# A transformer block, two spectral layers and a scan on one core: attention in query blocks of 464 columns, and position terms along w from slices of one table

## The chip, the core and the metric

The kernel runs on one core of a Trainium2 chip. TensorE (PE) multiplies matrices; VectorE (DVE), ScalarE (ACT) and GpSimd (POOL) work on elements; SyncE (SP) issues most of the transfers (DMA). The metric is the time of one execution on the device, in microseconds (us), lower is better. An f32 matrix product shows in the profile as two MATMUL instructions, a bf16 one as one.

## The reference, cut to what matters

The input is an image of 48 x 48 tokens with 768 channels, all f32. Four layers follow one another: an attention block with an MLP, a spectral mixing layer, a scan, and a second spectral layer. Only the attention of the first is touched:

```python
qkv = xn.reshape(B, H * W, C) @ qkv_w + qkv_b          # 12 heads of 64
attn = jnp.einsum('bqc,bkc->bqk', q * scale, k)         # 2304 x 2304 for a head
coords = jnp.arange(H)[:, None] - jnp.arange(H)[None, :] + (H - 1)
Rh = rel_pos_h[coords]
Rw = rel_pos_w[coords]
rel_h = jnp.einsum('bhwc,hkc->bhwk', r_q, Rh)
rel_w = jnp.einsum('bhwc,wkc->bhwk', r_q, Rw)
attn = (attn.reshape(B * nh, H, W, H, W) + rel_h[:, :, :, :, None] + rel_w[:, :, :, None, :])
attn = jax.nn.softmax(attn.reshape(B * nh, H * W, H * W), axis=-1)
out = jnp.einsum('bqk,bkc->bqc', attn, v)
```

The position term along w takes, for a query in column w, the dot product of q with 48 rows of a table of 95: `rel_pos_w[w - k + 47]`. For all queries of one column it is the same 48 rows, a window of the table that moves by one row from column to column. The term along h is built in the same way.

## The kernel before, in words

`qkv_phase` (L181) makes q, k and v for three superblocks (sb) of 768 tokens. For each superblock, `v_rows` makes v, then `q_and_k` (L268) goes over six pairs of heads (pr), each with seven matrix products of 128 x 128 weights (`wqk`, loaded from DRAM by `load_qk`, L243, for the second and third superblock), and stores q and k to DRAM on ACT's queue (L327).

Beside these runs the work on position terms, `position_terms` (L382). It is a list of steps, 24 for a superblock: twelve h steps (`rel_h`, L407), then twelve w steps (`rel_w`, L392). A step makes four products of 96 moving columns into one PSUM tile, and `split` (L367) turns it into three bf16 parts: ACT copies the first part (L371), VectorE subtracts (L372), ACT copies the second part (L373), VectorE subtracts (L374). The weights of each step are a table of 192 KB, `relD`, loaded by `tables` (L376); it holds for each of four positions a 128 x 96 block-diagonal matrix, so that one full-array product serves both heads of a pair. When the parts of a superblock are complete, `store` (L388) writes them to DRAM (`rw_d`, `rh_d`); the tiles `rw` and `rh` have one buffer each.

`advance` (L434) runs one step, and keeps the loads of the next ones ahead of it. It is called twice in each of the pairs 2 to 5 of `q_and_k` (L323; that makes the first eight h steps), and between the products of v of the next superblock (`between`, L444; the other sixteen). The third superblock has no v after it: its last sixteen steps run at the end, where a bound on the scores is computed as well (L461 to L478, ending in `flag`, by which the attention chooses between two programs; here it always takes `attention_bounded`). Four steps stand after the bound, then the pools of the projections are closed (`inner.close()`), five more follow, then `ahead(1)` opens the attention's buffers and loads its first block, and the rest of the steps follows. `ahead(0)`, which loads the one-hot table and the keys and values of the first pair of heads, stands after pair 1 of the last superblock (L329).

`attention_bounded` (L526) goes over six pairs of heads, for each over six blocks of 384 queries, for each over 18 tiles of 128 keys, in groups of three key tiles (`KB`). A group issues on TensorE, in this order: the products of keys and queries for its three tiles (L559; the two heads use the upper and the lower 64 rows of the array), the position terms added to them by a product with a 0/1 matrix `oneh` (L567, bf16, 120 rows), and the values of the group before (L588; the two heads use the left and the right 64 columns). ACT takes the exponential of each tile for both heads (L569), VectorE adds up the row sums (L574, L577). At the end of a block the sums are added over partitions (L595), inverted (L597) and multiplied in (L603). `load_bias` (L489) loads a block's position terms, with eight transfers for a pair of heads, and `load_chunk` loads q besides; two blocks are held (`qbs`). Every seventh group one step of `weight_sums` (L742) is run: it loads weights of later stages through SP, adds them on POOL and stores them. It borrows buffers from the pool of probabilities (`p`, ten buffers).

The instructions of an engine run in the order in which they are queued. The framework may place an instruction earlier or later than its line in the program, as long as what it depends on is done; SP's queue shows it most.

Of the kernel before, what the change touches and what calls it, by code (L numbers as in the profile page):

```python
# [20 lines left out]
P = 128  # L21
# [9 lines left out]
NTB = T // TB  # L31
LN_EPS = 1e-5
# [148 lines left out]
def qkv_phase(tc, ident, x, qkv_w, qkv_b, relT, rel_d, ln_g, ln_b, q_d, k_d, v_d, rw_d, rh_d, wqk_d, wv_d, flag, home, ahead):  # L181
# [18 lines left out]
    with (  # L200
# [67 lines left out]
        def q_and_k(sb, have_q, step):  # L268
# [4 lines left out]
            for pr in range(NC):  # L273
# [55 lines left out]
                if pr == 1 and sb + 1 == NSB:  # L329
                    ahead(0)  # L330
# [9 lines left out]
        with tc.tile_pool(name="qkv_v0", bufs=1, side="right") as vp:  # L340
            w = vp.tile([P, 7, NC2, TB], F32, tag="wv", name="wv")
            a21 = vp.tile([P, NC2, TB], F32, tag="a21", name="a21")
            load_x(0, 0)
            for k in range(2):
                nc.sync.dma_start(w[:, k], wv[:, k * NC2 : (k + 1) * NC2, 2 * C : 2 * C + TB])
            prepare(0, 0)
            load_x(0, 1)
            nc.sync.dma_start(w[:, 6], wv[:, NC2:, 2 * C + TB :])
            nc.sync.dma_start(a21, wv[:, :NC2, 2 * C + TB :])
            vb = load_bcast(nc, kp, qkv_b[2 * C : 3 * C], C, "vb")  # L350
            qkb = load_cols(nc, kp, qkv_b[0 : 2 * C], 2 * NC, "qkb")
            kb = kp.tile([P, NC], F32, tag="kb", name="kb")
            rel = qp.tile([P, 2, 2 * G - 1], F32, tag="rel", name="rel")
            for s in range(2):
                nc.sync.dma_start(rel[s * HD : (s + 1) * HD], relT)
            qms, kms = (qp.tile([P, NC, NSB], F32, tag=n, name=n) for n in ("qms", "kms"))
            prepare(0, 1)
            combine(nc.gpsimd, (w[:, 0], w[:, 1], a21, w[:, 6]), w[:, 3], w[:, 2], w[:, 5], w[:, 4])
            sums(0)
            V.tensor_scalar(kb, qkb[:, NC : 2 * NC], HD**-0.5, None, ALU.mult)  # L360
            v_rows(0, lambda n: w[:, n])
            nc.sync.dma_start(wv_d, w)

        with tc.tile_pool(name="qkv_o", bufs=1, side="right") as op:
            R = 2 * G

            def split(ps, parts, n):  # L367

                r = op.tile([P, TB], F32, tag="rest", name=f"rest_{n}", bufs=2)
                r = r[:R].rearrange("p (a b c) -> p a b c", a=ps.shape[1], b=ps.shape[2])  # L370
                nc.scalar.copy(parts[0], ps)  # L371
                V.tensor_tensor(r, ps, parts[0], ALU.subtract)  # L372
                nc.scalar.copy(parts[1], r)  # L373
                V.tensor_tensor(parts[2], r, parts[1], ALU.subtract)  # L374

            def tables(which, g, n):  # L376

                d = qp.tile([P, 4, R], F32, tag="relD", name=f"relD_{which}_{g}_{n}", bufs=4)
                nc.sync.dma_start(d, rel_d[which, g])
                return d  # L380

            def position_terms(sb, q):  # L382
# [5 lines left out]
                def store(d, at, cols):  # L388
                    for s in range(2):
                        nc.sync.dma_start(d[s, :, :, sb, cols], at[s * G : (s + 1) * G].rearrange("k n c b t -> k n (c b t)"))  # L390

                def rel_w(g):  # L392

                    if g == 0:
                        tiles["rw"] = op.tile([P, 3, NC, 2, TB], BF16, tag="rw", name=f"rw_{sb}")
                    d, at = tiles.pop(("w", g)), tiles["rw"]
                    ps = pm.tile([P, 512], F32, tag="m", name=f"rw_{sb}_{g}")
                    pv = ps[:R, :TB].rearrange("p (c b w h) -> p c b w h", c=NC, b=2, w=4)
                    j, w0 = divmod(4 * g, KTW)
                    for i in range(4):  # L400
                        nc.tensor.matmul(pv[:, :, :, i, :], lhsT=d[:, i, :], rhs=q6[:, :, :, j, w0 + i, :], start=True, stop=True)
                    cols = slice(j * P + w0 * KTH, j * P + (w0 + 4) * KTH)
                    split(ps[:R, :TB].rearrange("p (c b t) -> p c b t", c=NC, b=2), [at[:R, n, :, :, cols] for n in range(3)], f"w{sb}_{g}")
                    if g == G // 4 - 1:
                        store(rw_d, at, slice(0, NC * TS))

                def rel_h(cp, n, hh):  # L407
# [10 lines left out]
                    if (n, hh) == (1, 1):  # L418
                        store(rh_d, at, slice(2 * cp * TS, (2 * cp + 2) * TS))

                def load(key, *args):
                    tiles[key] = tables(*args, "_".join(str(k) for k in (sb, *key)))

                for cp in range(NC // 2):
                    for n in range(2):
                        for hh in range(2):
                            key = "h", cp, n, hh
                            steps.append((lambda key=key: load(key, 0, 2 * (2 * sb + key[2]) + key[3]), lambda key=key: rel_h(*key[1:])))
                for g in range(G // 4):
                    steps.append((lambda g=g: load(("w", g), 1, g), lambda g=g: rel_w(g)))  # L430
# [21 lines left out]
            for sb in range(NSB):  # L452
# [6 lines left out]
                q_and_k(sb, lambda q: position_terms(sb, q), advance)  # L459

# [4 lines left out]
            V.tensor_reduce(rm, rel, axis=AX.X, op=ALU.max, apply_absolute_value=True)  # L465
# [13 lines left out]
            for _ in range(4):  # L479
                advance()  # L480
            inner.close()
            for _ in range(5):
                advance()
# [5 lines left out]
def load_bias(nc, bt, rw_d, rh_d, h, blk):  # L489

    c, s = divmod(h, 2)
    nw = 3 * KTW
    sb, n = divmod(blk, 2)
    cols = slice((2 * c + n) * TB, (2 * c + n + 1) * TB)
    w = rw_d[s].rearrange("(j k) n b f -> j (k n) b f", j=KJ)[:, :, sb, cols].rearrange("j r t -> r j t")
    r = rh_d[s].rearrange("(a k) n b f -> a (k n) b f", a=2)[:, :, sb, cols]
    for a in range(2):
        nc.sync.dma_start(bt[:nw, a], w)
        nc.sync.dma_start(bt[nw:NBR, a], r[a].unsqueeze(1).to_broadcast([NBR - nw, KJ, TB]))
# [9 lines left out]
def attention_loads(nc, q_d, k_d, v_d, rw_d, rh_d):  # L509
# [7 lines left out]
    def chunk(qb, c):  # L517
        pr, qc = c
        nc.sync.dma_start(qb[0], q_d[pr * P : (pr + 1) * P, qc * TB : (qc + 1) * TB])
        for s in range(2):  # L520
            load_bias(nc, qb[1][:, s], rw_d, rh_d, 2 * pr + s, qc)
# [4 lines left out]
def attention_bounded(tc, ahead, oT, beside, load_next):  # L526
# [12 lines left out]
    QB = TB  # L539
    KB = 3  # L540
    (load_keys_values, load_chunk), kvs, qbs, ones, oneh = ahead
    with (
# [9 lines left out]
        probs, scs = {}, {}  # L552

        def products(c, kt):
            pr, qc = c
            ps = ps_s.tile([P, 2, 512], F32, tag="s", name=f"s_{pr}_{qc}_{kt}")
            for s in range(2):
                rows = slice(s * HD, (s + 1) * HD)
                nc.tensor.matmul(ps[:, s, :QB], lhsT=keys[pr % 2][rows, kt * P : (kt + 1) * P], rhs=qbs[qc % 2][0][rows], start=True, stop=False)  # L559
            scs[c, kt] = ps  # L560

        def scores(c, kt):
            pr, qc = c
            b, j = divmod(kt, KJ)
            ps = scs.pop((c, kt))
            for s in range(2):
                nc.tensor.matmul(ps[:, s, :QB], lhsT=oneh[:NBR, b % 3, :], rhs=qbs[qc % 2][1][:NBR, s, b // 3, j, :], start=False, stop=True)  # L567
            p = pp.tile([P, 2, QB], F32, tag="p", name=f"p_{pr}_{qc}_{kt}")
            nc.scalar.activation(p, ps[:, :, :QB], AF.Exp)  # L569
            probs[c, kt] = p  # L570

            if kt == 1:
                acc = rp.tile([P, 2, QB], F32, tag="acc", name=f"acc_{pr}_{qc}")
# [7 lines left out]
        def values(c, kt):  # L581
# [4 lines left out]
            for s in range(2):  # L586
                rows = slice(s * HD, (s + 1) * HD)
                nc.tensor.matmul(avs[c][rows, :QB], lhsT=vals[pr % 2][:, kt, rows], rhs=p[:, s, :], start=kt == 0, stop=kt == NT - 1)  # L588

        def row_sums(c):  # L590
            pr, qc = c
            acc = probs.pop(c)
            rs = ps_v.tile([P, 512], F32, tag="rs", name=f"rs_{pr}_{qc}")
            for s in range(2):
                nc.tensor.matmul(rs[s * HD : (s + 1) * HD, :QB], lhsT=ones, rhs=acc[:, s, :], start=True, stop=True)  # L595
            rec = rp.tile([P, QB], F32, tag="rec", name=f"rec_{pr}_{qc}")
            nc.vector.reciprocal(rec, rs[:, :QB])  # L597
            recs[c] = rec

        def finish(c):  # L600
            pr, qc = c
            av, rec = avs.pop(c), recs.pop(c)
            nc.vector.tensor_tensor(oT[:, pr, qc * QB : (qc + 1) * QB], av[:, :QB], rec, ALU.mult)  # L603

        work = [((pr, qc), k0) for pr in range(NC) for qc in range(T // QB) for k0 in range(0, NT, KB)]
        other = beside(op, lambda name: pp.tile([P, 2, QB], F32, tag="p", name=name))
        for i in range(len(work) + 1):
            if i % 7 == 3:
# [3 lines left out]
            if i < len(work):  # L612
                c, k0 = work[i]
                pr, qc = c
                if k0 == 0:
                    nxt = (pr, qc + 1) if qc + 1 < T // QB else (pr + 1, 0)
                    if nxt[0] < NC:
                        load_chunk(qbs[nxt[1] % 2], nxt)
# [18 lines left out]
def attention_any(tc, ident, oneh, q_d, k_d, v_d, rw_d, rh_d, oT, beside, load_next):  # L637
# [9 lines left out]
    with (  # L647
# [13 lines left out]
        for h in range(NH):  # L661
# [5 lines left out]
            for i in range(NTB):  # L667
                load_bias(nc, bt[:, :, :, i * TB : (i + 1) * TB], rw_d, rh_d, h, i)
# [623 lines left out]
def block_kernel(ctx: ExitStack, tc: tile.TileContext, a: dict):  # L1292
# [25 lines left out]
    def load_ahead(stage):  # L1318
# [7 lines left out]
        qbs = [(pool.tile([P, TB], F32, tag=f"qt{i}", name=f"qt{i}"), pool.tile([P, 2, 2, KJ, TB], BF16, tag=f"bt{i}", name=f"bt{i}")) for i in range(2)]  # L1326
# [462 lines left out]
def laid_out(i):  # L1789
# [9 lines left out]
    rel = np.zeros((2, G, 2, HD, 2 * G), np.float32)  # L1799
    for pos in range(G):  # L1800
        for s in range(2):
            rel[:, pos, s, :, s * G : (s + 1) * G] = d["relT"].transpose(1, 0, 2)[:, :, G - 1 - pos : 2 * G - 1 - pos]
    d["relD"] = rel.reshape(2, G // 4, 4, P, 2 * G).transpose(0, 1, 3, 2, 4)
# [34 lines left out]
```

## Time and profile before

| | |
|---|---|
| median of three runs | 3839.18 us (3835.62 to 3842.34) |
| the profiled execution | 3837.04 us |
| its span, first to last instruction | 3835.2 us |
| mean granted TensorE clock | 0.987 |
| projections and position terms (0 to 514 us) | 513.8 us |
| attention (514 to 1688 us) | 1174 us |
| position terms along w, MATMUL of L401 | x288, 32.6 us busy |
| position terms along h, MATMUL of L415 | x288, 55.8 us busy |

In the profile's group lines, a group is named by line, engine and operation, then output<-input by the program's names, the shape and the count; after the bar come the busy time in us and the mean of one instruction in ns, and after the second bar the idle time of the engine just before them, with what ended it. PEld is the weight load that goes with a MATMUL. A MATMUL's duration includes the way through the array, so two that follow each other overlap; the rate is read from start to start. In the timeline a line has the start, the time to the end of the last of the instructions merged in it, and in square brackets the idle time before it and what ended that. SPq lines are transfers as they are issued. The chain is the sequence of work that ended last.

### The profile page before, as it was taken

Reading aid. Unit: us, or ns where it says so; the run is one execution under the profiler, and the core shown is the slowest. Engines: PE = TensorE matmul, PEld = TensorE weight load, DVE = VectorE, ACT = ScalarE, POOL = GpSimd, SP = SyncE. Lnnn points to the kernel's source line nnn. Section 1 sums busy time; section 2 is a strip of 40 time slices with the busy share of each in tenths; the row PEclk is TensorE's granted clock in tenths of the full one; section 3 lists DMA queues with packets and bytes.
Section 4 is the critical chain, followed back from the end, with each engine's and each line's share of the span. In section 5 each row is a group of like instructions: output and inputs, shape, how many; then the busy total and the mean of one; then the engine's idle time right before and its main releaser. Section 6 shows DMA issues by size and latency. Waiting matters only on the chain.

```text
span 3835.2 us, 54419 instructions
## 1 busy us (share of the span) xinstructions
PE 3726.5 (97%) x22018; PEld 2254.6 (59%) x22018; DVE 2058.8 (54%) x3184; ACT 1146.8 (30%) x1911; POOL 655.8 (17%) x498
## 2 busy tenths in 40 slices
PE   8999979999999999999999999999999998999998
PEld 4666544444444444445555555555558876996685
DVE  6655456666666666555524332323325567995455
ACT  1322234444444444420310121012013356223342
POOL 3101001111111111015000000000013310982131
PEclk9999989999999999999999999999999999999999
DMA  7656563333232322124434533443453412112345
GB/s 256 213 188 192 180 186 120 112 105 126 87 114 76 113 77 91 42 71 133 154 107 137 173 104 114 136 146 105 124 160 102 113 41 94 36 36 73 97 116 154
DMA packets 267834, 460.43 MB, mean 120 GB/s; under 512 B 33053, under 2 KB 220373, under 8 KB 261079
## 3 DMA queue, kind: packets, MB, share of 16 engines
q1 hardware_dynamic: 257767, 435.93, 37.2%
q10 hardware_dynamic: 9808, 20.94, 1.5%
q8 instruction: 175, 2.87, 0.3%
q14 instruction: 84, 0.69, 0.1%
HBM read 318.49 MB, written 138.31 MB: 119 GB/s over the span
## 4 chain that ended last, share of the span: by engine, by line
PE 90%; DVE 3%; DMA 2%; POOL 2%; ACT 1%; issue 1%; SPq 0%; ACTq 0%; DVEq 0%; POOLq 0%
PE p L867 13%; PE p L930 13%; PE s L559 12%; PE av L588 12%; PE s L567 6%; PE qk L295 6%; PE c L1094 4%; PE c L1187 3%; PE v L164 3%; PE pj L164 2%; PE f_z L1497 2%; PE f_z L1498 2%; PE f_x L1462 2%; PE so L1272 2%; PE f_u L1512 2%; PE rh L415 1%
## 5 line engine op out<-in xcount | busy, mean ns | idle before, releaser
L577 DVE TENSOR_TENSOR acc<-acc,p 128x768 f32<-128x768 f32 x576 | 583.9, 1014 | 353.9 <-ACT p L569 315.7
L569 ACT ACTIVATE p<-s 128x768 f32<-128x768 f32 x648 | 478.5, 812 | 693.8 <-PE s L567 581.3
L930 PE MATMUL p<-w,h 128*128 128x384 f32 x1512 | 492.7, 486 | 0.0
L559 PE MATMUL s<-qt,kv 64*128 64x384 f32 x2592 | 478.5, 502 | 9.9 <-ACT p L569 7.7
L588 PE MATMUL av<-p,kv 128*64 128x384 f32 x2592 | 464.5, 493 | 0.0
L930 PEld LDWEIGHTS p<-w,h 128*128 128x128 f32 x1512 | 286.2, 190 | 196.9
L559 PEld LDWEIGHTS s<-qt,kv 64*128 64x128 f32 x2592 | 233.1, 187 | 250.6 <-ACT p L569 116.3
L588 PEld LDWEIGHTS av<-p,kv 128*64 128x64 f32 x2592 | 170.0, 136 | 225.2 <-issue 216.1
L867 PE MATMUL p<-x2nT,w 128*128 128x384 f32 x864 | 292.7, 488 | 3.9 <-POOL rr L906 3.9
L295 PE MATMUL qk<-xnT,wqk 128*128 128x384 f32 x756 | 252.4, 491 | 5.2 <-DMA wqk<-wqk_d 5.2
L1187 PE MATMUL c<-H,bands 128*48 128x96 f32 x5632 | 243.8, 247 | 11.1 <-issue 10.9
L567 PE MATMUL s<-bt,oneh 120*128 120x384 bf16 x1296 | 249.2, 329 | 0.0
L1187 PEld LDWEIGHTS c<-H,bands 128*48 128x48 f32 x5632 | 235.6, 124 | 19.5 <-issue 11.3
L867 PEld LDWEIGHTS p<-x2nT,w 128*128 128x128 f32 x864 | 164.8, 191 | 119.2 <-POOL rr L906 4.1
L867 PE MATMUL p<-xT,w 128*128 128x384 f32 x648 | 220.8, 486 | 0.0
L567 PEld LDWEIGHTS <-oneh 120*128 120x128 bf16 x1296 | 109.3, 98 | 174.6 <-issue 116.1
L295 PEld LDWEIGHTS qk<-xnT,wqk 128*128 128x128 f32 x756 | 144.6, 193 | 99.9 <-issue 8.5
L906 POOL TENSOR_TENSOR rr<-rr,ml_b 128x1152 f32<-128x1152 f32 x12 | 31.9, 2660 | 955.6 <-DMA rr<-xr_d 864.4
L862 ACT ACTIVATE h<-h,ml_b 128x384 f32<-128x384 f32 x144 | 88.4, 615 | 345.8 <-DVE h L882 174.3
L1195 POOL TENSOR_TENSOR t<-s,c 128x768 f32<-128x768 f32 x80 | 144.7, 1834 | 178.8 <-DMA bands<-in_bands_dram 169.1
L867 PEld LDWEIGHTS p<-xT,w 128*128 128x128 f32 x648 | 123.1, 190 | 85.9
L597 DVE RECIPROCAL rec<-rs 128x384 f32<-128x384 f32 x36 | 92.1, 2558 | 100.7 <-PE rs L595 100.7
(322 smaller groups left out, 4803.7 us busy)
## 6 DMA issues: line engine op xcount, KB each, us to landing
w<-w1s_d SPq DMA_DIRECT2D x36, 768.0 KB
w<-w2s_d SPq DMA_DIRECT2D x36, 768.0 KB
bt<-rh_d SPq DMA_DIRECT2D x144, 162.0 KB
w<-w1s_d SPq DMA_DIRECT2D x36, 576.0 KB
w<-in_mlp_w_dram SPq DMA_DIRECT2D x27, 768.0 KB
wqk<-wqk_d SPq DMA_DIRECT2D x12, 1344.0 KB
yu<-f_ys SPq DMA_DIRECT2D x24, 672.0 KB
bt<-rw_d SPq DMA_DIRECT2D x144, 108.0 KB
```

Of the source, the lines that this page charges most:

```text
L164: nc.tensor.matmul(p[:, :TB], lhsT=rhs[n][:, c, t * P : (t + 1) * P], rhs=w[:, c, :], start=c == 0, stop=c == NC2 - 1)
L295: nc.tensor.matmul(p[:, :TB], lhsT=w[:, n, c, :], rhs=ops[sb][n][:, c, :], start=c == 0, stop=c == NC2 - 1)
L559: nc.tensor.matmul(ps[:, s, :QB], lhsT=keys[pr % 2][rows, kt * P : (kt + 1) * P], rhs=qbs[qc % 2][0][rows], start=True, stop=False)
L567: nc.tensor.matmul(ps[:, s, :QB], lhsT=oneh[:NBR, b % 3, :], rhs=qbs[qc % 2][1][:NBR, s, b // 3, j, :], start=False, stop=True)
L569: nc.scalar.activation(p, ps[:, :, :QB], AF.Exp)
L577: nc.vector.tensor_tensor(probs[c], probs[c], p, ALU.add)
L588: nc.tensor.matmul(avs[c][rows, :QB], lhsT=vals[pr % 2][:, kt, rows], rhs=p[:, s, :], start=kt == 0, stop=kt == NT - 1)
L867: nc.tensor.matmul(p[:, :TB], lhsT=w[n][:, c, :], rhs=rhs[n][:, c, :], start=c == 0, stop=c == NC2 - 1)
L930: nc.tensor.matmul(ps[t][:, :TB], lhsT=hs[left, f][:, t * P : (t + 1) * P], rhs=wt[:, f % KW2, :], start=f == 0, stop=f == NF2 - 1)
L1094: nc.tensor.matmul(ps[:K, i, :n], lhsT=v[:, c, tok : tok + K], rhs=w[:, cc, c0 : c0 + n], start=cc == NC - 1, stop=cc == 0)
L1187: nc.tensor.matmul(ps[r0 : r0 + G, k // 4, cols], lhsT=bands[:, n - GC, i, :] if gr else bands0[:, n, i, :], rhs=H[:, n, :, d : d + NPR], ...
L1195: GP.tensor_tensor(t, sc[:, ch], c1[:, m0 : m0 + GC].unsqueeze(2).to_broadcast([P, GC, RR, NPR]), ALU.mult)
```

## The change

- The attention's query block has 464 columns (`QB`) for 384: 2304 queries make four blocks of 464 and one of 448. A block may reach over the border of two superblocks (tokens 768 and 1536), and `load_bias` then loads it in two parts, with sixteen transfers for eight. Buffers and slices take the new size; the two held blocks alternate over all blocks.
- Every sixth group, for every seventh, runs a step of `weight_sums`.
- The w steps load no table. Their weights are slices of 64 columns of one table `rel` on chip, which was there for the bound (95 columns; now padded to 111). As the slice has no block-diagonal form, each position takes two products, one for each head, with 64 rows and 64 columns of the array: rows and outputs 0 to 63 for the first, 64 to 127 for the second. `rw` has 128 partitions in use, of which 48 + 48 are stored.
- The order of a superblock's steps is eight h, four w, four h, eight w.
- Six of the last steps stand ahead of the bound; then come the bound, `inner.close()`, `ahead(1)` and the ten others.
- `ahead(0)` stands after pair 3 of the last superblock, for pair 1.

```diff
+QB = 464
+NQB = -(-T // QB)
...
-                if pr == 1 and sb + 1 == NSB:
+                if pr == NC2 and sb + 1 == NSB:
                     ahead(0)
...
-            rel = qp.tile([P, 2, 2 * G - 1], F32, tag="rel", name="rel")
+            rel = qp.tile([P, 2, G - 1 + HD], F32, tag="rel", name="rel")
+            V.memset(rel[:, :, 2 * G - 1 :], 0.0)
...
                 def rel_w(g):
...
-                    pv = ps[:R, :TB].rearrange("p (c b w h) -> p c b w h", c=NC, b=2, w=4)
+                    pv = ps[:, :TB].rearrange("p (c b w h) -> p c b w h", c=NC, b=2, w=4)
                     j, w0 = divmod(4 * g, KTW)
                     for i in range(4):
-                        nc.tensor.matmul(pv[:, :, :, i, :], lhsT=d[:, i, :], rhs=q6[:, :, :, j, w0 + i, :], start=True, stop=True)
+                        k0 = G - 1 - (4 * g + i)
+                        for s in range(2):
+                            rows = slice(s * HD, (s + 1) * HD)
+                            nc.tensor.matmul(pv[rows, :, :, i, :], lhsT=rel[rows, 1, k0 : k0 + HD], rhs=q6[rows, :, :, j, w0 + i, :], start=True, stop=True)
...
-                for g in range(G // 4):
-                    steps.append((lambda g=g: load(("w", g), 1, g), lambda g=g: rel_w(g)))
+                w = [(lambda: None, lambda g=g: rel_w(g)) for g in range(G // 4)]
+
+                steps.extend(h[:8] + w[:4] + h[8:] + w[4:])
...
                 q_and_k(sb, lambda q: position_terms(sb, q), advance)
+            for _ in range(6):
+                advance()
...
-            for _ in range(4):
-                advance()
             inner.close()
-            for _ in range(5):
-                advance()
             ahead(1)
             while steps or ready:
                 advance()
...
+    at = t0
+    while at < t0 + n:
+        sb, t = divmod(at, 2 * TB)
+        m = min(2 * TB - t, t0 + n - at)
+        cols = slice(2 * c * TB + t, 2 * c * TB + t + m)
+        dst = bt[:, :, :, at - t0 : at - t0 + m]
...
+        for a in range(2):
+            nc.sync.dma_start(dst[:nw, a], w)
+            nc.sync.dma_start(dst[nw:NBR, a], r[a].unsqueeze(1).to_broadcast([NBR - nw, KJ, m]))
+        at += m
+
+def queries(qc):
+    return slice(qc * QB, min(T, (qc + 1) * QB))
...
-        work = [((pr, qc), k0) for pr in range(NC) for qc in range(T // QB) for k0 in range(0, NT, KB)]
+        work = [((pr, qc), k0) for pr in range(NC) for qc in range(NQB) for k0 in range(0, NT, KB)]
...
-            if i % 7 == 3:
+            if i % 6 == 3:
                 next(other, None)
```

## The prediction

> **What bounds the kernel now.** I read the page first, its busy rows and its costliest groups:
>
> ```profile
> PE 3726.5 (97%) x22018; PEld 2254.6 (59%) x22018; DVE 2058.8 (54%) x3184; ACT 1146.8 (30%) x1911; POOL 655.8 (17%) x498
> L569 ACT ACTIVATE p<-s 128x768 f32<-128x768 f32 x648 | 478.5, 812 | 693.8 <-PE s L567 581.3
> L559 PE MATMUL s<-qt,kv 64*128 64x384 f32 x2592 | 478.5, 502 | 9.9 <-ACT p L569 7.7
> L588 PE MATMUL av<-p,kv 128*64 128x384 f32 x2592 | 464.5, 493 | 0.0
> L567 PE MATMUL s<-bt,oneh 120*128 120x384 bf16 x1296 | 249.2, 329 | 0.0
> ```
>
> TensorE is busy for 97%, and in the attention (562 to 1688 us) the windows view gives 1126.00 busy of 1126.00. So only TensorE's own work, or its few idle places, can give time back. I then took the timeline of TensorE in the middle of the attention:
>
> ```profile
> 901.00 2.21 PE L559 MATMUL s<-qt,kv 64*128 64x384 f32 x12
> 903.14 1.15 PE L567 MATMUL s<-bt,oneh 120*128 120x384 bf16 x6
> 904.22 2.16 PE L588 MATMUL av<-p,kv 128*64 128x384 f32 x12
> 906.30 2.21 PE L559 MATMUL s<-qt,kv 64*128 64x384 f32 x12
> ```
>
> The reader should see one group of three key tiles every 5.30 us: products 2.14, position terms 1.08, values 2.08 (from start to start). How much of it is columns? A long run elsewhere, p L930 x258 in 83.20 us of the chain, gives 0.3225 us for one f32 instruction of 384 columns. Durations of 486 ns at 384 columns (L930) and 247 at 96 (L1187) give 0.83 ns a column, thus 0.320 of columns and 0.0025 of issue. Bf16 takes one pass for two, 0.1625. Products and values run their two heads in pairs (six slots for twelve instructions). So a group is 12 x 0.3225 + 6 x 0.1625 = 4.845 us, and 0.457 us of the measured 5.302 is neither columns nor issue. The weight loads of the same timeline show where it sits: inside the values they come every 0.32 us (904.59, 904.92, 905.24, 905.56), but from the first values pair (904.22) to the next is 0.37, and from the last (905.88) to the products (906.30) is 0.42. It is paid when the array changes its shape: about 0.10 to drain, and 0.05 to load 64 columns of weights uncovered (twice that for 128).
>
> Last, the waits of TensorE outside the steady part, by the timeline at the end of the projections:
>
> ```profile
> 478.30 2.12 PE L295 MATMUL qk<-xnT,wqk 128*128 128x384 f32 x6
> 483.86 0.20 PE L475 MATMUL bound<-pz,onec 128*1 128x12 f32 x2 [3.44 <-DVE pz L471]
> 483.99 5.91 PE L415 MATMUL rh<-q,relD_h 128*96 128x96 f32 x32
> 489.72 2.22 PE L401 MATMUL rw<-q,relD_w 128*96 128x96 f32 x24
> 492.42 0.89 PE L401 MATMUL rw<-q,relD_w 128*96 128x96 f32 x8 [0.48 <-DMA relD_w<-in_relD_dram]
> 496.49 3.76 PE L401 MATMUL rw<-q,relD_w 128*96 128x96 f32 x24 [3.18 <-DVE rw L374]
> 506.44 5.26 PE L401 MATMUL rw<-q,relD_w 128*96 128x96 f32 x40 [6.19 <-DMA relD_w<-in_relD_dram]
> 513.83 2.21 PE L559 MATMUL s<-qt,kv 64*128 64x384 f32 x12 [2.13 <-DVE rest_w L372]
> 551.55 1.01 PE L559 MATMUL s<-qt,kv 64*128 64x384 f32 x2 [5.99 <-ACT p L569]
> ```
>
> From the last projection (ends 480.4) to the attention (513.8) are 33.4 us with some 14 us of TensorE work in them.
>
> **The change part by part**, against the profiled execution (3837.0; its span 3835.2 and 1.8 around it; the median of the three runs, 3839.2, is 2.1 above).
>
> *464 columns.* 36 blocks of 6 groups become 30: four of 464 and one of 448 columns for each pair of heads. A slot of 464 columns is 464 x 0.833 ns = 0.3867, + 0.0025 = 0.389, its bf16 one 0.196; a group is 12 x 0.389 + 6 x 0.196 + 0.457 = 6.302, one of 448 is 6.102. A pair of heads costs 24 x 6.302 + 6 x 6.102 = 187.86 against 36 x 5.302 = 190.87. Row sums: two slots for each block, 3.87 both ways. Six pairs: **-18.1 us**. It is simply 36 changes of shape (of groups) fewer. The other end is 0, if the 0.457 grew with the columns; the even 0.32 inside each kind speaks against that. ScalarE and VectorE scale along: three exponentials 3 x 0.98 and three sums 3 x 1.23 (812 and 1014 ns by 928/768) against 6.30; the reciprocal of 2558 ns becomes 3.1 us in a block of 38, and the next block's first values come a group later. The longer block loads are hidden: in the timeline of SP, a block's last load is issued at 1024.63, and it is first read at 1041.5 (blocks are 32.45 us apart). Blocks 2 and 4 of each pair cross a 768-token border and issue 17 loads for 9; 8 x 0.42 us and 21% more bytes take 5 of these 17 us, and 38-us blocks give 3 back. Without cover it would be those 5 us, 12 times. The weight sums step every 6 groups of 6.3 for 7 of 5.3: the same pace, done by group 171 of 180.
>
> *w terms by halves.* A step was 8 instructions (0.68 us: 369.09 to the next v at 369.77); it becomes 16, of 64 rows by 64 columns, 96 moving columns each. If the two halves run together, as L1187's column halves do (96 columns, x2752 in 118.65 us of the chain, 43 ns each where L401 takes 85), the step stays at 0.68. But it now stands as a change of shape between full-array matmuls: in 0.10 + 0.05, out 0.10 + 0.10, 0.35 us. 24 steps stand in the v stages, where TensorE is busy without a break (60.96 of 61 us at 320 to 381): **+8.4 us**. The other 12 stand in the tail, below.
> [...] By the row (L1187 and the values put two column tiles into one bank and overlap) +8.4. I take the row, since these tiles too lie on separate output partitions. Ends: 0 (the drains hide) and +24.7; a gain is excluded, as the moving columns stay the same.
> The split works on 128 partitions for 96: 475 ns on 96 (L371) and 479 on 128 (L871) for the same columns, so nothing. The pad memset, the sliced maximum and the host table cost nothing that is waited for.
>
> *Fewer loads, later keys.* 36 table loads of 192 KB leave SP's queue. The wait of 5.2 us of qk for wqk at 398.4 has its load issued at 381.01 and landing 17.3 later, with the first pair's v (1152 KB) in front since 373.40. Moved behind the fourth pair of projections, that v should come later: 1.18 MB at that stretch's 250 GB/s is 4.7 us. **-4 us** (0 to -5.2; the later place meets only the sixth pair's weights, loaded at 431.4 for use 30 us later).
>
> *The tail.* The h casts wait there until 488.6 for a store (ScalarE idle 6.74 before them), and everything behind is queued; then come table loads. Now four w steps come first, with neither wait, and fill those 8.2 us. The other 12 steps go at VectorE's pace, two passes of 0.55, 1.13 us each: 13.6. With 1.5 of handing over it is 8.2 + 13.6 + 1.5 = 23.3 for 33.4: **-10 us**. Ends: -14 (all 16 at that pace, 18 us, no store waited for) and 0 (the first block's loads, 1.54 MB at some 200 GB/s, take its place; issued at about 490 they land at about 498, before the 502 when they are wanted). The bound now waits behind six steps, but its flag is wanted only at the attention.
>
> *The stall at 545.* The exponential of the sixth group waits for a buffer that holds a weight block; POOL frees it at 550.7, 36.8 us after the attention's start, and it was due 29 after. Due is now 34; 8 more loads on SP and more bytes put the block 3 to 5 later. **-1 us** (-6 to +3).
>
> Sum: -18.1 + 8.4 - 4 - 10 - 1 = -24.7 on 3837.0 gives 3812.3, and on the median's footing **3814**.
>
> **The rivals.**
> A, as above: 72%, own range 3802 to 3824 (tail and stall by their ends, drains hidden or not).
> B, the halves share a bank and go one after the other: +16.3 in the v stages, and 12 x 0.25 in the tail, where TensorE (1.4 us a step) now outruns VectorE's 1.13: -5.4, about 3834. [...] against it the overlapping column tiles. 12%.
> C, slower: the array drains between the two halves every time, as it does between products and values. Each of 16 instructions is then 0.08 + 0.10 + 0.05 = 0.23 us, a step 3.7: +72 in the v stages and a tail of some 50 for 33, with -23 elsewhere, about +66: 3905. It decides from 2.05 us a step: 24 (x - 0.68) + (12 x + 5.6 + 2 - 33.4) - 23 = +8 gives it. Against it: row halves and column halves each overlap without a drain. 4%.
> D, the opening gives nothing: the first blocks' transfers take the place of the waits removed (the DMA share there is 0.5 to 0.8). -18.1 + 8.4 = -9.7, about 3829. 8%.
> E, 464 columns do not do what they say: the 0.457 grows with the columns, -6.6, about 3832. 4%.
>
> **How the numbers follow.** Three runs spread by 0.2%; about 0.2%, 7.7 us, is what a measurement can tell, so faster means under 3831.5. Faster: A 0.72, most of D 0.06, some of B and E 0.07, together 0.85; within 0.2%: the rest of B, D and E, 0.11; slower: C, 0.04. The range 3799 to 3834 holds A, D, half of B and most of E, over 8 in 10.
>
> **What would show it.** In the attention, groups of 6.30 us with 0.42 still from the last values pair to the products: the columns are right; 6.40 would be E. L401's new line: 1.03 us from its first instruction to the next v matmul (A), 1.7 (B), over 2 (C). The wait on wqk near 398 under 1.5 us; no wait of PE on relD; last projection to first product about 23 us. I would be wrong most of all if the w halves don't overlap, or if the scheduled order on SP sets a new wait in the tail.

## The result, and the profile after

The changed kernel takes 3823.84 us (median of seven runs, 3819.09 to 3825.16) against 3839.18: a ratio of 0.9962, with a 95% interval of 0.9953 to 0.9972. It is 15.3 us faster; 3814 was predicted, with a range of 3799 to 3834. Its profiled execution took 3819.09 us, the shortest of its seven, with a span of 3817.3, so its profile shows 18.0 us of gain and the medians 15.3. Parts are compared by the profiles, whole kernels by the medians and ratios.

From the page of the changed kernel:

```profile
PE 3715.2 (97%) x21202; PEld 2163.4 (57%) x21202; DVE 2028.6 (53%) x3071; ACT 1137.4 (30%) x1803; POOL 652.2 (17%) x498
...
L587 ACT ACTIVATE p<-s 128x928 f32<-128x928 f32 (+1 forms) x540 | 467.9, 939 | 682.9 <-PE s L585 576.9
...
L576 PE MATMUL s<-qt,kv 64*128 64x464 f32 (+1 forms) x2160 | 471.6, 569 | 11.3 <-DVE rest_w L376 6.2
L606 PE MATMUL av<-p,kv 128*64 128x464 f32 (+1 forms) x2160 | 456.3, 557 | 0.0
```

The same columns go through in 2160 instructions for 2592, and the busy time falls by 7 and 8 us in these two kinds. The busy times of different kinds overlap, so the gain of a group can't be read from them. It is read from start to start, in the timeline of TensorE in the attention:

```profile
529.51 2.61 PE L576 MATMUL s<-qt,kv 64*128 64x464 f32 x12
532.05 1.35 PE L585 MATMUL s<-bt,oneh 120*128 120x464 bf16 x6
533.33 2.56 PE L606 MATMUL av<-p,kv 128*64 128x464 f32 x12
535.81 2.60 PE L576 MATMUL s<-qt,kv 64*128 64x464 f32 x12
```

A group now lasts 6.30 us from products to products (529.51 to 535.81), as worked out. The price of a change of shape stands where it stood: inside the values the weight loads come every 0.39 us (534.16, 534.55, 534.93), and from the last of these to the products are 0.88, which is two such slots and 0.10 (before: 0.74 from 905.56 to 906.30, two slots of 0.32 and 0.10).

Where the last superblock's q and k begin and where the attention ends, first in the kernel before and then in the changed one:

```profile
379.47 13.71 PE L295 MATMUL qk<-xnT,wqk 128*128 128x384 f32 x42
1692.78 1.46 PE L588 MATMUL av<-p,kv 128*64 128x384 f32 x6
```

```profile
383.09 13.71 PE L297 MATMUL qk<-xnT,wqk 128*128 128x384 f32 x42
408.40 4.14 PE L297 MATMUL qk<-xnT,wqk 128*128 128x384 f32 x6 [11.60 <-DMA wqk<-wqk_d]
1674.10 1.67 PE L606 MATMUL av<-p,kv 128*64 128x448 f32 x6
```

By stretches, from the starts and ends in the two timelines (the attention is counted here to its last product, 6 us beyond the 1688 of the table for the kernel before):

| stretch | before | after | change | predicted |
|---|---|---|---|---|
| up to the last superblock's q and k | 379.5 | 383.1 | +3.6 | +8.4 |
| the last superblock's q and k | 100.9 | 106.4 | +5.5 | -4 |
| from there to the attention | 33.4 | 24.1 | -9.3 | -10 |
| attention | 1180.4 | 1162.1 | -18.3 | -19.1 |
| all that follows | 2141.0 | 2141.5 | +0.5 | 0 |

One line of it went the wrong way. The waits of TensorE between 375 and 575 us, with the total, the number and the longest:

```profile
PE qk L297 <- DMA wqk<-wqk_d: 11.6, 1, 11.6
PE s L576 <- DVE rest_w L376: 6.2, 1, 6.2
PE s L576 <- ACT p L587: 5.1, 2, 3.3
```

The wait on `wqk`, 5.2 before, was to go and has more than doubled. SP's queue ahead of it:

```profile
376.01 0.57 SPq L528 DMA_DIRECT2D kv<-v_d  x1
376.63 2.88 SPq L394 DMA_DIRECT2D rw_d<-rw  x2
380.82 2.82 SPq L236 DMA_DIRECT2D v_d<-v_o  x1
383.77 3.68 SPq L247 DMA_DIRECT2D wqk<-wqk_d  x1
```

The load of the first pair's v, which was moved behind pair 3 in the program, is still issued ahead of the weights; it depends on nothing that comes later, and was queued as early as before. The other waits are at the opening of the attention:

```profile
487.40 2.12 PE L297 MATMUL qk<-xnT,wqk 128*128 128x384 f32 x6
489.45 2.86 PE L408 MATMUL rw<-q,rel 64*64 64x96 f32 x64
...
506.54 0.88 PE L408 MATMUL rw<-q,rel 64*64 64x96 f32 x16 [0.24 <-DVE rest_w L376]
513.67 4.82 PE L576 MATMUL s<-qt,kv 64*128 64x464 f32 x12 [6.25 <-DVE rest_w L376]
...
521.51 4.30 PE L576 MATMUL s<-qt,kv 64*128 64x464 f32 x12 [1.74 <-ACT p L587]
...
558.11 4.16 PE L576 MATMUL s<-qt,kv 64*128 64x464 f32 x12 [3.32 <-ACT p L587]
```

The tail has no wait on a table any more, and VectorE sets its pace (steps 1.12 us apart). But TensorE, done at 507.4, idles for 6.25 us at its end, and three groups of products take 4.2 to 4.8 us where 2.6 is the rule. The granted clock is 0.52 from 513.7 to 518.4 us, the first of the three, and 0.62 in the other two (521.5 to 526.0, 558.1 to 562.4); this is the half clock spoken of below.

### The profile page after: what moved, and what is told of

Its sections match the earlier page's. It is cut to its first block, busy times and chain, and to the rows that moved or that the text cites. A ratio compares the mean times of both kernels' runs of the same rounds, so it can differ in the third digit from the quotient of the medians.

```text
span 3817.3 us, 52324 instructions
## 1 busy us (share of the span) xinstructions
PE 3715.2 (97%) x21202; PEld 2163.4 (57%) x21202; DVE 2028.6 (53%) x3071; ACT 1137.4 (30%) x1803; POOL 652.2 (17%) x498
## 4 chain that ended last, share of the span: by engine, by line
PE 87%; DVE 5%; DMA 3%; POOL 2%; ACT 2%; issue 1%; SPq 1%; ACTq 0%; DVEq 0%; POOLq 0%
PE p L886 13%; PE p L949 13%; PE s L576 12%; PE av L606 11%; PE qk L297 6%; PE s L585 6%; PE c L1113 4%; PE v L166 3%; PE pj L166 2%; PE f_z L1516 2%; PE f_z L1517 2%; PE f_x L1481 2%; PE so L1291 2%; PE f_u L1531 2%; PE rh L422 1%; DVE s L1226 1%
## 5 line engine op out<-in xcount | busy, mean ns | idle before, releaser
L595 DVE TENSOR_TENSOR acc<-acc,p 128x928 f32<-128x928 f32 (+1 forms) x480 | 561.3, 1169 | 361.0 <-ACT p L587 329.7
L587 ACT ACTIVATE p<-s 128x928 f32<-128x928 f32 (+1 forms) x540 | 467.9, 939 | 682.9 <-PE s L585 576.9
L576 PE MATMUL s<-qt,kv 64*128 64x464 f32 (+1 forms) x2160 | 471.6, 569 | 11.3 <-DVE rest_w L376 6.2
L606 PE MATMUL av<-p,kv 128*64 128x464 f32 (+1 forms) x2160 | 456.3, 557 | 0.0
L576 PEld LDWEIGHTS s<-qt,kv 64*128 64x128 f32 x2160 | 195.5, 188 | 282.5 <-issue 167.3
L606 PEld LDWEIGHTS av<-p,kv 128*64 128x64 f32 x2160 | 141.9, 136 | 247.2 <-issue 237.8
L297 PE MATMUL qk<-xnT,wqk 128*128 128x384 f32 x756 | 251.6, 490 | 11.6 <-DMA wqk<-wqk_d 11.6
L1206 PE MATMUL c<-H,bands 128*48 128x96 f32 x5632 | 244.5, 247 | 11.1 <-issue 10.9
L585 PE MATMUL s<-bt,oneh 120*128 120x464 bf16 (+1 forms) x1080 | 241.5, 360 | 0.0
L585 PEld LDWEIGHTS <-oneh 120*128 120x128 bf16 x1080 | 90.9, 98 | 192.1 <-issue 111.7
L616 DVE RECIPROCAL rec<-rs 128x464 f32<-128x464 f32 (+1 forms) x30 | 91.1, 3038 | 98.9 <-PE rs L614 98.9
```

Of the source, the lines that this page charges most:

```text
L297: nc.tensor.matmul(p[:, :TB], lhsT=w[:, n, c, :], rhs=ops[sb][n][:, c, :], start=c == 0, stop=c == NC2 - 1)
L576: nc.tensor.matmul(ps[:, s, :n], lhsT=keys[pr % 2][rows, kt * P : (kt + 1) * P], rhs=held(c)[0][rows, :n], start=True, stop=False)
L585: nc.tensor.matmul(ps[:, s, :n], lhsT=oneh[:NBR, b % 3, :], rhs=held(c)[1][:NBR, s, b // 3, j, :n], start=False, stop=True)
L587: nc.scalar.activation(p, ps[:, :, :n], AF.Exp)
L595: nc.vector.tensor_tensor(probs[c], probs[c], p, ALU.add)
L606: nc.tensor.matmul(avs[c][rows, : size(c)], lhsT=vals[pr % 2][:, kt, rows], rhs=p[:, s, :], start=kt == 0, stop=kt == NT - 1)
```

## The experiments

The question was where the missing gain lies: what lengthens the wait on `wqk`, and what the attention's opening costs. Each kernel was timed beside the kernel before on the same chip; the second time given is that kernel's median there. Kernels timed on different chips are compared by their ratios to it.

**464 columns alone** (`qkv_phase` and its tables as in the kernel before):

> The kernel before with blocks of 464 columns and their loads alone; position terms, their order, the tail and the place of the keys' load as before. Theory: 36 groups' changes of shape fewer, 18 us, and 0 to 3 us of the stall at the sixth group: 18 to 21 us under the kernel before (0.9950). Rival (the 0.46 us that a group costs beyond its columns grows with the columns): 7 us or less is left of a gain (0.998).

Measured: 3814.55 against 3836.72, ratio 0.9944 (0.9931 to 0.9958). That is 22 us, more than the whole change gave. The attention took 1158.3 us for 1180.4; the sixth group waits 3.4 us there for 6.0. The groups' share is the 18 us of the sum, and the 1.5 left over would be less of the half clock after that wait, by my estimate (in the kernel before, the granted clock is 0.50 from 551.5 to 556.5 us); the rival falls.

**W terms, order and tail alone** (`QB = TB`, weight sums every seventh group):

> The changed kernel with blocks of 384 columns and the weight sums every seventh group, as before; w terms from the table on chip, new order of steps and new place of the keys' load stay. Theory: 24 w steps at +0.30 us (+7), the wait on wqk +6, the tail -9: 3 to 5 us over the kernel before (1.001). Rival (the on-chip w terms and the tail gain by themselves): 0 to 5 us under it.

Measured: 3840.58 against 3836.72, ratio 1.0010 (1.0002 to 1.0019), 3.9 us slower. So the second half of the change takes away a part of what the first gives.

**The place of the keys' load:**

```diff
-                if pr == NC2 and sb + 1 == NSB:
+                if pr == 1 and sb + 1 == NSB:
                     ahead(0)
```

> The changed kernel with one edit undone: the keys and values of the first pair are loaded after pair 1 of the last superblock again. Theory: that place put the keys' load, which waits 9.8 to 12.9 us on SP for a store of k, ahead of the load of the third pair's weights, and so kept that load away from the second pair's; with the new place both weight loads (1344 KB each) move at once, and the wait of qk on wqk grew from 5.2 to 11.6 us. Then the wait is 5 to 6 us again and the time 5 to 7 us under the changed kernel's (about 3818, 0.9945 of before). Rival: the wait grew from the other traffic (v stores, the store of rw, the values' load, which is still ahead of it); then the wait stays at 10 to 12 us and the time at 3824.

Measured: 3822.24, ratio 0.9960 (0.9946 to 0.9974); the wait is 10.9 us. My first theory fell: the keys' load stands in front of the third pair's weights again (in the kernel before it waits 12.9 us for the store of k, until 400.40, and SP issues those weights behind it at 400.81), and nothing changes beyond the noise (0.9962 for the changed kernel).

**Keys and values held back** (a copy from the maxima that pair 3 leaves goes into two columns of their tile first):

> The changed kernel, with the first pair's keys and values held back for real: a copy of two columns of the maxima that pair 3 leaves goes into their tile first, so that neither load can be placed ahead of it. Theory (two weight loads at once): the values' 1152 KB leave the road of the second pair's weights, the third pair's stay on it; the wait on wqk falls from 11.6 to about 6 us, time 5 us under the changed kernel's. Rival (the values' load in front decides): the wait falls under 1 us and the time by 11 us. If the loads now fall into the end of the projections and hold up the first block, part of that comes back there.

Measured: 3818.34, ratio 0.9955 (0.9941 to 0.9968), wait 7.8 us. Moving that load away in earnest gives 4 us of waiting, as the prediction had it for the original move; but 7.8 remain, more than the 5.2 of before. Neither theory gave that number. The time is not clear of the changed kernel's.

In the transfer records of the trace the store of w terms moves in packets of 9216 bytes. The store of the first superblock's terms, which runs during the second superblock's q and k, has 288 of them; they take 628 ns each and 15.3 us in all before, and 763 ns and 20.2 us after. The store that stands ahead of the wait, one superblock later, can be told apart from the load of v (which has packets of the same size) only where the keys and values are held back: 764 ns and 20.2 us. That led to the next two.

**Rows apart** (464 columns alone, loaded tables, full-array products; the second head's block of the w table moved from column 48 to 64). The edit is not quite alone: all loaded tables grow from 96 to 112 columns (192 to 224 KB each), and a w step takes 0.77 us for 0.68:

```diff
-            rel[:, pos, s, :, s * G : (s + 1) * G] = d["relT"].transpose(1, 0, 2)[:, :, G - 1 - pos : 2 * G - 1 - pos]
+            for n, apart in enumerate((G, HD)):
+                rel[n, pos, s, :, s * apart : s * apart + G] = d["relT"][:, n, G - 1 - pos : 2 * G - 1 - pos]
```

> The kernel with 464 columns alone, and one thing of the w terms: the loaded table has its second head's block at columns 64 to 111, so that the full-array products leave the rows on partitions 0 to 47 and 64 to 111, and the store reads them there; no product by halves. Theory (where the rows lie makes the store slow): the store packets take about 760 ns, the wait on wqk 10 to 12 us for 5.4, the time 5 to 7 us over that kernel's (ratio 0.996). Rival (the products by halves, through their timing, are behind it): packets at 630 ns, wait at 5 us, time at 0.9945.

Measured: 3835.44 against 3838.14, ratio 0.9996 (0.9988 to 1.0005): 20 us of the 22 are gone, three times what I expected. The packets take 762 ns, as expected. Its waits of TensorE from 240 to 580 us, the longest line:

```profile
PE qk L297 <- DMA wqk<-wqk_d: 16.1, 2, 12.1
```

There are now two waits on `wqk`, 12.1 as expected and 4.0 in the superblock before. Set against the profile of 464 columns alone, the wait of 12.1 for 5.4 is 6.7 of the 20 us; the wait of 4.0 and what follows it are 6, the wider w products are 2, the attention is 3 slower (1.5 of it a longer wait at the sixth group, 4.9 for 3.4), and 3 lie after the attention, where nothing was changed. That the other 2 of the 6 and 1.5 of the 3 are half clock is an estimate, from the 0.87 and 0.62 that follow such waits in the changed kernel. So about 7 us belong to the question. The wait of 4.0, which the changed kernel doesn't have, may come from the wider tables too; that was not separated. For the wait of 12.1 they hardly count: the four tables loaded just ahead of it are 128 KB larger together, half a microsecond by my estimate, at the 252 GB/s of the next view. The stretches of the first superblock's store, with the last two columns the share of the transfer engines' time and what they moved (GB/s), in the kernel with 464 columns alone:

```profile
221.50:237.10 15.60, 15.60 (x50) 9.17 (x49) 4.49 (x9) 1.09 (x2) 5.24 (x2) 1.00 0.99 252
```

and with the rows apart:

```profile
221.70:242.10 20.40, 19.82 (x67) 11.71 (x66) 7.77 (x15) 2.99 (x6) 5.25 (x2) 1.00 0.96 226
```

The transfer engines are nearly as busy as before and move a tenth less. Where the rows lie is enough to make the store slow, without any product by halves; and as the changed kernel loads no w tables and has the same 763 ns, the wider tables are not the cause of that.

**The store held back** (in the changed kernel; `z` is zero times a maximum of pair 2, so the store can't be queued earlier):

```diff
+                if pr == 2 and late:
+                    at, put = late.pop()
+                    z = qp.tile([P, 1], F32, tag="z", name="z")
+                    V.tensor_scalar(z, kms[:, pr, sb : sb + 1], 0.0, None, ALU.mult)
+                    e = at[:, :, NC - 1, 1, TB - 1 : TB].rearrange("p a b -> p (a b)")
+                    V.tensor_scalar(e, e, z, None, ALU.add)
+                    put()
```

> The changed kernel with the store of the second superblock's w terms (two transfers of 1296 KB) held back until pair 2 of the last superblock, by an addition of zero that needs that pair's maxima. The place of the keys' load is out as a cause. Theory now: in the changed kernel the rows of w terms lie on partitions 0 to 47 and 64 to 111, its store packets of 9216 bytes take 763 ns for 628 and the store 20.2 us for 15.3, and that stands in the road of the second pair's weights. Then the wait on wqk falls from 11.6 to 0 to 2 us, and the time by 8 to 10 us under the changed kernel's (ratio to before about 0.994). Rival (the values' load and the stores of v do it alone): the wait stays over 7 us.

Measured: 3806.37 against 3838.14, ratio 0.9922 (0.9909 to 0.9936), by the ratios some 15 us under the changed kernel for the 8 to 10 expected, with no wait on `wqk` at all: its waits from 375 to 575 us begin with

```profile
PE s L586 <- ACT p L597: 6.9, 2, 5.2
PE s L586 <- DVE rw L386: 6.3, 1, 6.3
```

The load of v still stands in front (376.02); without the store it harms nobody. The last superblock's q and k take 92.6 us for 106.4, 13.8 less for a wait of 11.6. After the wait the changed kernel ran at a granted clock of 0.87 from 408 to 425 us, and this one at 1.00 from 383 to 420. I had left this share out of what I expected.

**TensorE kept busy ahead of the attention** (20 products of the identity, never read):

> The changed kernel with 20 products of the identity with itself, never read, after the last position step. In the changed kernel TensorE idles 6.25 us before the attention, and the first two product groups take 4.8 and 4.3 us for 2.6. Theory: the idle time brings the granted clock down, and the attention's first groups pay 3.9 us for it; with TensorE at work the groups take 2.6 and the time falls by 3 to 4 us (ratio 0.9952). Rival (the slow first groups have another cause, as the first block's data landing late): they stay at 4 to 5 us, and the time too or 1 us up.

Measured: 3821.5, ratio 0.9963 (0.9949 to 0.9976), no gain. The stretch of the attention's first 10 us (the clock is the third number from the right), in the changed kernel:

```profile
513.60:523.60 10.00, 8.19 (x24) 3.67 (x26) 1.80 (x3) 4.09 (x5) 0.00 (x0) 0.67 0.82 171
```

and with TensorE kept busy:

```profile
514.00:524.00 10.00, 8.23 (x38) 3.33 (x40) 3.00 (x5) 5.14 (x7) 0.00 (x0) 1.00 0.82 172
...
558.33 4.96 PE L579 MATMUL s<-qt,kv 64*128 64x464 f32 x12 [6.97 <-ACT p L590]
```

(the last line is from its timeline). The mechanism was right: the clock is 1.00 and the first groups take 2.6 and 2.7 us. But the products after the sixth group begin at 558.33 for 558.11. The 4 us won were waited off there, by 6.97 us for 3.32. So the gap of 6.25 us in the changed kernel cost 4 us of clock, and these 4 counted only once the next wait was out of the way. A gap of 1.74 us stands before the second group in both kernels: after it the products take 4.30 us in the changed kernel and 2.72 with TensorE kept busy, so the length of one gap alone doesn't tell.

**The first weight block later** (`if i % 6 == 3 and i > 3`, in the changed kernel):

> The changed kernel with the first step of the weight sums at the attention's tenth group for its fourth. Theory: the sixth group's exponential waits for a buffer that a weight block holds, and that block comes 44.4 us after the attention's start whatever else is done (44.4 in the changed kernel, 44.3 with TensorE kept busy, 44.5 with the store held), since SP's transfers, the store of w terms first, set it; without the block there is no stall at the sixth group: 3.3 us of waiting and the half clock after it (some 2 us) go, 4 to 6 us under the changed kernel. Rival: the stall only moves to a later group, where the same block is waited for; time as the changed kernel's.

Measured: 3816.59 against 3837.32, ratio 0.9951 (0.9937 to 0.9964). The products after the sixth group, in its timeline:

```profile
554.58 2.61 PE L576 MATMUL s<-qt,kv 64*128 64x464 f32 x12
```

No wait stands before them, at 41.1 us after the attention's start for 44.4, and none came later. By the profiles it is 4.7 us under the changed kernel.

**All three** (store held, TensorE busy, block later):

> The changed kernel with three edits that take away waits: the store of w terms held back, TensorE kept busy ahead of the attention by 20 products never read, and the first weight block later. Theory: the busy TensorE gave nothing alone because the sixth group's stall took its 4 us; with the stall gone it counts: 16 (store) + 5 (stall) + 4 (clock) under the changed kernel, about 3798 to 3801 (ratio 0.990). Rival (the parts overlap, so no more than the store's 16 remains): 3806, 0.992.

Measured: 3798.82, ratio 0.9901 (0.9885 to 0.9916). The attention took 1153.2 us for 1162.1. The parts add up, and the 4 us of the clock count now.

**Tables kept, but loaded early** (464 columns, full-array w products, new order and tail, eight table buffers):

> The kernel with 464 columns alone, w terms still from loaded tables by full-array products and stored from partitions 0 to 95, but in the new order of steps and the new tail, with eight buffers for the tables for four and loads seven steps ahead for three. Theory: the tail gets its 9 us from the order and from not waiting for tables, whoever holds them; no changes of shape (7 us) and no slow store (6 us) are paid: 8 to 10 us under the 464-alone kernel, 0.992. Rival (the tables' loads compete with the first block's there): the tail gains under 4 us, 0.9935 or more.

Measured: 3808.18 against 3838.14, ratio 0.9932 (0.9919 to 0.9946). The tail took 26.9 us, 6.5 less than in the kernel before for the 9 expected: 6.1 us of waits on tables remain, since four of the last eight are issued behind the first block's loads. By the ratios it is 4 to 5 us under 464 columns alone for the 8 to 10 expected. Still, with tables kept it is faster than the changed kernel (0.9962).

**And with the store held and the block later:**

> The kernel with 464 columns and w terms from loaded tables by full-array products, in the new order and tail with tables loaded seven steps ahead; besides, the store of the second superblock's w terms held back and the first weight block later. Theory: it pays neither the 7 us of changes of shape nor the slow store, nor the wait on wqk (about 8 us with its half clock): 3798 to 3801 (0.990), level with the one of three edits or a little under. Rival (the held store meets the tables' loads at the end and brings waits there): 3806 or more, 0.992.

Measured: 3795.78 against 3837.32, ratio 0.9890 (0.9875 to 0.9906), the lowest of all, though not clear of the three edits (0.9901); its waits from 375 to 600 us:

```profile
PE rw L411 <- DMA relD_w<-in_relD_dram: 7.8, 3, 7.1
PE s L580 <- DVE rest_w L382: 2.8, 1, 2.8
PE s L580 <- ACT p L591: 1.5, 1, 1.5
```

TensorE waits 7.8 us for tables that the changed kernel doesn't load at all, and it is still level with the three edits: it pays neither the 24 changes of shape nor the wait on `wqk`. Of the change, the 464 columns and the order of steps earned the time; taking the w weights from the chip did not show a gain in any run here.

## Why the prediction was right, and where it was not

*464 columns, -18.1.* Right, and for the reason given. The group has 6.30 us by the trace, and the price of 0.46 us beyond columns and issue didn't grow with the columns. The bf16 slot of 0.1625 us is borne out by the kernel before: six of L567 last 1.15 us together and one 0.326, so they start 0.165 apart. The 0.05 for 64 columns of weights is in the weight loads too, which take 136 ns for 64 columns (L588) and 187 for 128 (L559). That the 0.10 is the array draining was an estimate from the starts; the traces show the time, not what fills it.

*W terms by halves, +8.4.* Right in mechanism, a little too dear. In the v stages of the changed kernel:

```profile
354.86 0.88 PE L408 MATMUL rw<-q,rel 64*64 64x96 f32 x16
355.67 2.20 PE L166 MATMUL v<-wv,xnT 128*128 128x384 f32 x6
357.80 0.88 PE L408 MATMUL rw<-q,rel 64*64 64x96 f32 x16
```

One w step and one v product last 2.94 us, 2.64 before (342.51 to 345.15): +0.30 for a step, 0.35 predicted, 7.2 for the 24. The step itself takes 0.81 from its start to the next v, so the halves run together, on separate output partitions of one PSUM tile. One after the other (rival B, 0.68 more for each of the 24 steps, with the 8.4 the +24.7 of the ends) would be 1.7; no trace of the kernel before spoke for it. Rivals B and C are out. The stretch grew by only 3.6, partly by luck, since 2.7 us of waits in the transposes of the second superblock and a stretch at a clock of 0.84 (195 to 206 us; 1.00 in the changed kernel) are gone. What ended these was not tried.

*Fewer loads, later keys, -4.* This step failed; it came out at +5.5. "Moved behind the fourth pair of projections, that v should come later" was wrong, since a line's place does not move a load that nothing holds. And the load was not what lengthened the wait: held back for real, it takes 4 us off, and 7.8 remain. What I priced at nothing was the row placement of `rw`: I costed `split` on 128 partitions, but not the store that reads from partitions 64 to 111. It takes 20.2 us for 15.3, in the road of the weights. With the rows apart and no product by halves the wait is 12.1 us, and with the store held back it is 0. Had I known it, this step would have stood at +5.5 and the sum 9.5 us higher.

*The tail, -10.* Right: 24.1 us for the 23.3 worked out, so rival D is out. But I left out that the idle end of a shorter tail would meet the attention's first groups: 4 us of half clock (0.67 on average in the first 10 us), inside the attention's number.

*The stall at the sixth group, -1.* The wait fell by 2.7, within the ends given. My reading that the block's arrival sets it held: TensorE goes on 44.4, 44.3 and 44.5 us after the attention's start in three kernels with different starts (the changed one, TensorE kept busy, store held), and after 40.8 and 40.6 in the two kernels with 464 columns and loaded tables, where the rows of the store lie together. But the small net is partly luck. Both of its terms moved further than I said, and nearly cancelled: the arrival by 6.7 us (37.7 before) for the 3 to 5 forecast, and the time when the block was due to 38.6 us after the start for the 34 forecast, since the half clock held up the groups ahead of it. With 464 columns alone the arrival moved by 3.1, as forecast.

The predicted time was 10 us below the median, and 6.8 below the profiled execution (3812.3 for 3819.1). The step that failed makes 9.5 of that; the v stages, 4.8 cheaper than forecast, hid half of it. That step was read from the program's lines rather than from what would be queued, and left out the store.

## What to carry to other kernels

Where every change of array shape costs a fixed price (here 0.46 us in a group of three), wider columns pay by the number of changes saved, and the trace of before gives that price. When a change moves data to other partitions, cost the transfers that read it there, and ask whom they delay. A load left its place in the queue here only when something that it needs came later, and a gain ahead of a wait that is set by an arrival (here 4 us, at the sixth group) counts only when the arrival moves too.

## What the runs showed of the hardware that I had not expected

A store of 2 x 48 rows (packets of 9216 bytes) took 628 ns a packet from partitions 0 to 47 and 48 to 95, and 763 ns from 0 to 47 and 64 to 111. These are the first superblock's stores; over all traces it is 626 to 630 and 762 to 769 ns. The store is two transfers, one for each head. In order of start, the first 144 packets take 712 ns before and 719 after, the second 144 take 545 before and 808 after. So the difference lies in the second half of the packets; by that order these are the second head's, whose rows are the ones that moved. Why they are read more slowly from partitions 64 to 111 than from 48 to 95 was not shown.
